# Two pairs of PSUM banks for the norm transposes, and the last image's query tiles from last to first, in a three-stage fp32 kernel

## The chip, the cores and the metric

The kernel runs on one core of one Trainium2 chip. The time is the device time of one execution in microseconds. Five engines work from queues of their own: TensorE (PE; PEld is its weight load), VectorE (DVE), ScalarE (ACT), GpSimd (POOL) and SyncE (SP), which here only issues DMA transfers. Each engine takes its instructions in the order of the program and waits at an instruction until the semaphores that it names have their value.

## The reference, cut to what matters

The input has 8 images of 256 channels and 32 x 32 pixels, all in fp32. A first layer (convolution, attention and a Fourier feed-forward part) is not touched by the change. Its result, as 1024 tokens per image, goes through a causal attention and a mixture of 8 experts:

```python
t = _to_tokens(x)                       # 8 x 1024 x 256
t = t + attention(_ln_t(t), WQ, WK, WV) # causal softmax over 1024 keys; scores equal to 0 are left out
u = _ln_t(t)                            # layer norm over the 256 channels
feat = mean(u, axis=0)                  # over the 8 images
w = softmax(feat @ Wr + br)             # a weight per token and expert
h = relu(bn(u @ W1[e])); h = relu(bn(h @ W2[e]))
y = sum_e w[e] * (h @ Wo[e] + bo[e])
x = _from_tokens(t + y)
```

The gate w needs the mean over all images, so no expert's result can be weighted before the last image's layer norm is done for those tokens.

## The kernel before, in words

Images lie channel-first: a tile t holds 2 x 128 channels (KC = 2) by 1024 tokens. The tokens are cut into two halves of 512 (HALF), eight query tiles of 128 (P) and four pairs of query tiles of 256 columns (QC).

**Layer 1's attention** (1428 to 2051 us of the span). For image b the main strand `causal` takes the query tiles 0 to 7. `scores` does eight matmul records' worth of 128x512 fp32 products into a tile s, VectorE takes the maximum (nm), and ScalarE the exponential (pr) over the causal width, 128 columns for tile 0 and 1024 for tile 7. `follow` then moves older tiles along: `norm` masks and sums on VectorE and scales on GpSimd; `turn` transposes pr on TensorE into banks "tp" and ScalarE copies them to pT; `product`, once per pair of query tiles, multiplies with the values (po), and VectorE adds po to t. The side strand `beside` runs, meanwhile, the first layer norm of image b+1, some splitting of expert weights ("chores"), the second layer norm of image b-1, and keys and values of image b+1 (pk, pv). `together` weaves the two strands by the costs that each `yield` names; this fixes the order of the program, and each engine follows it.

A layer norm (`layer_norm`, L1287) transposes pairs of token tiles on TensorE (tpt), copies them on ScalarE (zt), takes mean and variance on VectorE, the inverse root in six small steps on GpSimd, scales zt on VectorE two tiles at a time, transposes back in groups of four (tpz), and copies to z on ScalarE. For the second norm GpSimd adds the result to feats (two halves), and the result is split in parts and stored in z_d for layer 2.

PSUM in this stage: ps_s holds two score tiles (two banks each), ps_t two banks with the tag "tp", ps_m two banks with the tag "mm". pk, pv and po use "mm"; the transposes of pr use "tp". The norms and the gate take theirs from `bank`, which gives "tp" only:

```python
        def bank(shape, name):
            return ps_t.tile(shape, F32, tag="tp", name=name)
```

For the last image (b = 7) the side strand has no next image: it does the second norm of image 6, then `last_norm`, which waits until the pairs 0 and 1 are done, normalises the first half of image 7 (z2_last), adds it to feats[0], and runs `gate(0)`: logits (lg), softmax (ge) and a transpose (pwT) to wT. The second half of image 7 is normalised and gated later, inside layer 2 (`last_half`, L1822).

**Layer 2, the experts** (2051 to 3187 us). A visit is (group of four experts G, half h, image b). Each visit has four pieces, one per expert slot; a piece runs layer1 (pa, then h), two pieces later layer2 (pm), and four pieces after its start layer3 (q), so three layers run side by side. Each fp32 product is done in parts, with weights split before in wd. In the first visits of a half the gate's rows (pw) and the weighted bias (pg, `gated_bias`) are made as well. The pool `hp` and three PSUM pools open when the attention's pools close; a tile there lies over memory that the attention used. Weights are loaded by `load_expert`, tokens' parts by `fetch_z`, t by `fetch_t` (L1686), all through SP's queue in the order of the program.

Nearly all instructions of these layers carry the line of one recording helper (L72), so the profile is read by tile names.

Of the kernel before, what the change touches and what calls it, by code (L numbers as in the profile page):

```python
# [104 lines left out]
def conv_attn_hybrid_kernel(  # L105
# [1128 lines left out]
    brs = wm.tile([1, NE], F32, name="brs")  # L1234
    nc.sync.dma_start(brs, br)
    wT = wm.tile([4 * NE, N], F32R, name="wT")
    feats = [None, wm.tile([P, KC, HALF], F32, name="feat1")]
    z2_last = wm.tile([P, KC, HALF], F32, name="z2_last")
    mhalf1 = wm.tile([P, NT], F32, name="mhalf1")
    nc.gpsimd.memset(mhalf1, -0.5)  # L1240
# [124 lines left out]
    with ExitStack() as l1:  # L1365
# [19 lines left out]
            return w_  # L1385

        wv_s = load_w("wv", wvT)
        feats[0] = wpool.tile([P, KC, HALF], F32, name="feat0")
        load_t(1)


# [19 lines left out]
        def expert_parts():  # L1411

            for e in range(NE):
                for l, src in enumerate((w1, w2, wo)):
                    if not in_parts(e, l):
                        continue
                    w_ = two.tile([P, KC, C], F32, tag="we", name="we", bufs=1)
                    nc.sync.dma_start(w_, src[e].rearrange("(k p) o -> p k o", p=P))
                    yield
                    upper(parts_w, w_, dve)  # L1420
                    lower_part(parts_w, w_)
                    difference(parts_w)
                    dve.tensor_scalar_mul(parts_w[:, 1], parts_w[:, 1].bitcast(F32), STEP)
                    yield
                    nc.sync.dma_start(w_d[e][l], parts_w.bitcast(F32))
                if e == 0:
                    for k in range(3):
                        load_expert(wm, 0, k)

            consts["bn1"] = bn_fold("g1", "be1", "m1", "v1", eps_moe, "bn1", extra="b1")  # L1430
            consts["bn2"] = bn_fold("g2", "be2", "m2", "v2", eps_moe, "bn2", extra="b2")
            for i in "12":
                for x, f in (("a", 1.0 + 1.0 / STEP), ("b", -1.0 / STEP)):
                    consts[i + x] = const.tile([P, KC * NE], F32, name=f"s{i}{x}")
                    dve.tensor_scalar_mul(consts[i + x], consts["bn" + i][0], f)
            yield
            bo4 = tiny.tile([P, KC, 4, NE], F32, name="bo4", bufs=1)
            stacked(bo4, cols("bo").rearrange("p (e g) -> p g e", g=KC), (0, 0, 1, 1))
            pb = bank([4 * NE, KC, P], "pbo")
            for g in range(KC):  # L1440
                pe.transpose(pb[:, g, :], bo4[:, g].rearrange("p a e -> p (a e)"), ident)
            dve.tensor_copy(boT, pb)
            yield
            zs[0] = wm.tile([P, 3, KC, HALF], F32R, name="z_first")
            nc.sync.dma_start(zs[0].bitcast(F32), z_d[0][:, 0])
            load_expert(wm, 1, 0)
            yield

# [5 lines left out]
        def room(shape, tag, bufs):  # L1454
            return tiny.tile(shape, F32, tag=tag, name=tag, bufs=bufs)

        def bank(shape, name):
            return ps_t.tile(shape, F32, tag="tp", name=name)

        def rows_of_zt():  # L1460
# [56 lines left out]

        def last_norm():

            yield from until((B - 1, HALF // QC - 1))  # L1520
            yield from layer_norm(t[B - 1][:, :, :HALF], z2_last, rows_of_zt(), room, bank)
            dve.tensor_add(feats[0], feats[0], z2_last)
            nc.sync.dma_start(u_d[B - 1][:, :, :HALF], t[B - 1][:, :, :HALF])
            yield 0.5

        done, late, ready, turns, pr_of, pT = set(), [], [], [], {}, {}
        nq = QC // P

        def causal(b):
            for i in range(NT):  # L1530
                yield from scores(b, i)
                yield from follow()

        def follow():
            if ready:
                yield from product(*ready.pop(0))
            if late:
                norm(*late.pop(0))
            if len(turns) > 2 or (turns and not late and turns[0][0] == B - 1 and ended):
                b, i = turns.pop(0)  # L1540
                yield from turn(b, i)
                if i % nq == nq - 1:
                    ready.append((b, i // nq))

        def scores(b, i):
# [26 lines left out]
        def turn(b, i):  # L1572

            qc, qt = divmod(i, nq)
            if qt == 0:
                pT[b, qc] = two.tile([P, NT, QC], F32, tag="pT", name="pT1")
            pr = pr_of.pop((b, i))
            for j0 in range(0, i + 1, 4):
                jn = min(4, i + 1 - j0)
                tp = ps_t.tile([P, 4, P], F32, tag="tp", name="tp")  # L1580
                for j in range(jn):
                    pe.transpose(tp[:, j, :], pr[:, (j0 + j) * P : (j0 + j + 1) * P], ident)
                act.copy(pT[b, qc][:, j0 : j0 + jn, qt * P : (qt + 1) * P], tp[:, :jn, :])
                yield 0.12 * jn
# [18 lines left out]
        def beside(b):  # L1603

            def chore(n):
                for _ in range(n):
                    next(chores, None)
                    yield 1.0

            if b + 1 < B:  # L1610
                yield from first_norm(b + 1)
            yield from chore(3)
            if b >= 1:
                yield from second_norm(b - 1)
            yield from chore(2)
            if b + 1 < B:
                yield from keys_values(b + 1)
            else:
                yield from last_norm()
                yield from gate(0, room, bank)  # L1620
            yield from chore(2)

        def last():
# [12 lines left out]
            together(last() if b == B - 1 else causal(b), beside(b), 0.85)  # L1636
        for _ in chores:
            pass
        nc.sync.dma_start(u_d[B - 1][:, :, HALF:], t[B - 1][:, :, HALF:])

# [9 lines left out]


    with ExitStack() as l2:
        hp = l2.enter_context(tc.tile_pool(name="hp", bufs=2))
        ps_a = l2.enter_context(tc.tile_pool(name="ps_a2", bufs=2, space=PSUM))
        ps_b = l2.enter_context(tc.tile_pool(name="ps_b2", bufs=2, space=PSUM))
        ps_q = l2.enter_context(tc.tile_pool(name="ps_q2", bufs=1, space=PSUM))
        (s1, o1), (s2, o2) = consts["bn1"], consts["bn2"]
        s1a, s1b, s2a, s2b = (consts[x] for x in ("1a", "1b", "2a", "2b"))  # L1660

        visits = [(G, h, b) for G in range(NG) for h in range(2) for b in range(B)]
        pieces = [(v, s) for v in range(len(visits)) for s in range(SLOTS)]
        ts, gate_of, bias_of, h1_of, h2_of, acc_of = {}, {}, {}, {}, {}, {}

# [3 lines left out]
        def fetch_z(v):  # L1669
            if v < len(visits):  # L1670
                G, h, b = visits[v]
                zs[v] = hp.tile([P, 3, KC, HALF], F32R, tag="z", name="ze")
                if (G, b) == (0, B - 1):
                    parts, src = zs[v], z2_last if h == 0 else scratch[:, 2]
                    soon[0].append(lambda: upper(parts, src))
                    soon[1].append(lambda: lower_part(parts, src))
                    soon[2].append(lambda: difference(parts))
                    soon[3].append(lambda: later.append(lambda: nc.sync.dma_start(z_d[b][:, h], parts.bitcast(F32))))
                else:
                    nc.sync.dma_start(zs[v].bitcast(F32), z_d[b][:, h])  # L1680
# [120 lines left out]
                            nc.sync.dma_start(to, t)  # L1801
                    yield

        load_expert(hp, 1, 1)
        fetch_t(0)
        for s in range(1, SLOTS):
            for l in range(3):
                if (s, l) not in w_in:
                    load_expert(hp, s, l)
        fetch_z(1)  # L1810
        LAG2, LAG3 = 2, 4
        later = []
        scratch = hp.tile([P, 3, KC, HALF], F32, name="scratch", bufs=1)
# [7 lines left out]

        def last_half():  # L1822

            nc.sync.dma_start(scratch[:, 0], u_d[B - 1][:, :, HALF:])
            yield
            zt = scratch[:, 1].rearrange("p k (i c) -> p (k i) c", c=C)
            yield from layer_norm(scratch[:, 0], scratch[:, 2], zt, room2, bank2)
            dve.tensor_add(feats[1], feats[1], scratch[:, 2])
            yield
            yield from gate(1, room2, bank2)  # L1830

        extra = last_half()
        for n in range(len(pieces) + LAG3):
            one_ = two_ = three = iter(())
            if n < len(pieces):
                v, s = pieces[n]
                G, h, b = visits[v]
                if s == 1:
                    fetch_t(v + 1)
                    if v >= 1:  # L1840
                        fetch_z(v + 1)
                if s == 2 and G == 0:
                    dve.tensor_add(ts[v], ts[v], bias_of[h])
                one_ = layer1(v, s)
            if 0 <= n - LAG2 < len(pieces):
                two_ = layer2(*pieces[n - LAG2])
            if n >= LAG3:
                three = layer3(*pieces[n - LAG3])

            now, soon = soon, [[] for _ in range(4)]  # L1850
            for i in range(4):
# [8 lines left out]
            later.clear()  # L1860
            if n < len(pieces) and b == 0:
                gate_rows(G, h, s)
                if G == 0 and s < KC:
                    gated_bias(h, s)
            for l, lag in enumerate((0, LAG2, LAG3)):
                if 0 <= n - lag < len(pieces):
                    v, s = pieces[n - lag]
                    if visits[v] == (0, 1, B - 1):
                        load_expert(wm if s == 0 or (s, l) == (1, 0) else hp, SLOTS + s, l)


# [112 lines left out]
```

## Time and profile before

| | us |
|---|---|
| median of 3 runs | 3188.72 (3186.95 to 3191.35) |
| the profiled execution | 3188.79 |
| its span | 3186.8 |
| mean granted clock of TensorE | 0.966 |
| TensorE busy, 1500 to 1900 us | 379.9 of 400 |
| TensorE busy, 1963 to 2051 us (image 7 and gate) | 74.81 of 88 |
| TensorE busy, 2051 to 2100 us | 45.75 of 49 |
| TensorE busy, 2100 to 3100 us | 999.64 of 1000 |
| first scores of images 0 to 7 | 1463.76, 1517.44, 1590.68, 1665.03, 1739.31, 1813.63, 1889.42, 1963.73 |
| first matmul of layer 2 | 2050.89 |

In the lists of waits a line reads: engine and tile that waited, the engine and tile waited for, the sum in us, how often, and the longest. In the order of time a line gives start, duration, engine, line, operation, the tiles out and in, sizes, the number of instructions, and in brackets the idle time before them with what ended it. In tables by stretch each engine has its busy time and, in brackets, the count of its instructions.

### The profile page before, as it was taken

The page shows a single profiled execution, that of the slowest core. Times are in us where ns is not written, and L with a number is a line of the kernel's source. Part 1 is how long each engine was busy: PE and PEld are TensorE (multiplying, and loading weights), DVE is VectorE, ACT ScalarE, POOL GpSimd, SP SyncE. Part 2 cuts the span into 40 slices and gives each one's busy share as a digit, 9 for nine tenths or more (in the row PEclk, how much of TensorE's full clock was granted, in tenths as well). Part 3 has the DMA queues.
Part 4 walks back from the last instruction along what each step waited for, and adds up shares of the span by engine and source line. Part 5 has one row for each costly group of instructions (what it writes and reads, how often), then busy time and mean ns, then how long its engine had stood idle before and what let it go on. Part 6 is the DMA issues. An engine that isn't in the chain of part 4 may idle for free.

```text
span 3186.8 us, 41632 instructions
## 1 busy us (share of the span) xinstructions
PE 2936.5 (92%) x16802; PEld 1934.3 (61%) x16802; DVE 2390.5 (75%) x3014; ACT 1567.0 (49%) x2312; POOL 340.3 (11%) x419
## 2 busy tenths in 40 slices
PE   5998898998998989858999999799999999999998
PEld 3654555554555555435666666577777777777776
DVE  1378778878787879664677765588988888888887
ACT  1554445555554536323333332365666666666665
POOL 1121212111111110001222221100000000000000
PEclk9998999999999999979999999899999999999999
DMA  5213030302121120002433221322212242221220
GB/s 152 60 22 80 27 80 27 80 28 73 35 58 50 40 54 8 17 22 93 149 119 119 106 103 67 145 85 81 73 67 71 75 172 86 95 70 66 92 75 27
DMA packets 63854, 234.85 MB, mean 74 GB/s; under 512 B 5590, under 2 KB 13862, under 8 KB 54822
## 3 DMA queue, kind: packets, MB, share of 16 engines
q1 hardware_dynamic: 63654, 232.12, 21.9%
q8 instruction: 134, 2.20, 0.3%
q14 instruction: 66, 0.54, 0.1%
HBM read 140.61 MB, written 91.49 MB: 73 GB/s over the span
## 4 chain that ended last, share of the span: by engine, by line
PE 46%; DVE 6%; ACT 2%; issue 1%; DMA 0%; POOL 0%; SPq 0%; ACTq 0%; DVEq 0%; POOLq 0%
PE pm L72 12%; PE pa L72 11%; PE q L72 11%; PE s L72 4%; PE po L72 3%; PE pv L72 2%; PE pk L72 1%; DVE nm L72 1%; DVE zt L72 1%; DVE pr L72 1%; ACT pr L72 1%; PE tpz L72 1%; PE tpt L72 1%; DVE st L72 1%; PE tp L72 1%
## 5 line engine op out<-in xcount | busy, mean ns | idle before, releaser
L72 PE MATMUL pa<-ze,w 128*128 128x512 f32 x1488 | 423.1, 393 | 0.0
L72 DVE SCALAR_TENSOR_TENSOR x<-hpad,vec,x 128x1024 f32<-128x1024 f32 x248 | 317.0, 1282 | 40.7 <-ACT x L72 33.7
L72 DVE SCALAR_TENSOR_TENSOR conv<-hpad,vec,conv 128x1024 f32<-128x1024 f32 x256 | 329.2, 1293 | 13.8 <-ACT conv L72 7.3
L72 PEld LDWEIGHTS pa<-ze,w 128*128 128x128 f32 x1488 | 278.2, 188 | 63.3 <-issue 3.3
L72 ACT ACTIVATE h<-pa,bn_o,s1a 128x512 f32<-128x512 f32 x256 | 198.8, 777 | 204.5 <-PE pa L72 204.5
L72 ACT ACTIVATE pT<-s 128x1024 f32<-128x1024 f32 x256 | 247.5, 1025 | 71.6 <-PE s L72 71.6
L72 PE MATMUL po<-pT,vT 128*32 128x256 f32 x4096 | 272.6, 384 | 0.0
L72 PE MATMUL q<-h2p,w 128*128 128x512 f32 x768 | 269.8, 460 | 0.1
L72 DVE SCALAR_TENSOR_TENSOR h<-pa,s1b,h 128x512 f32<-128x512 f32 x256 | 191.2, 747 | 97.1 <-PE pa L72 86.6
L72 PE MATMUL ph<-xn,piw 128*128 128x512 f32 x512 | 245.2, 616 | 3.1 <-DVE xn L72 1.6
L72 PE MATMUL pm<-h,w 128*128 128x512 f32 x512 | 243.6, 598 | 0.0
L72 PE MATMUL s<-kk,z 128*128 128x512 f32 x512 | 241.3, 603 | 1.0 <-DVE pr L72 0.6
L72 PE MATMUL q<-z_first,w 128*128 128x512 f32 x768 | 216.1, 390 | 2.7 <-DVE z_first L72 1.7
L72 PE MATMUL pm<-h1p,w 128*128 128x512 f32 x768 | 216.1, 389 | 0.5 <-DVE h1p L72 0.5
L72 DVE SCALAR_TENSOR_TENSOR o<-vpad,pe_w,o 128x1024 f32<-128x1024 f32 x128 | 163.5, 1282 | 45.8 <-ACT o L72 42.7
L72 PEld LDWEIGHTS q<-h2p,w 128*128 128x128 f32 x768 | 144.7, 189 | 84.3 <-issue 60.1
L72 PE MATMUL s<-qst,kst 128*128 128x256 f32 x1024 | 176.3, 314 | 14.9 <-DMA kst<-part 13.5
L72 ACT ACTIVATE hpad<-ph,pi_o 128x512 f32<-128x512 f32 x126 | 86.9, 690 | 183.0 <-PE ph L72 182.9
L72 PEld LDWEIGHTS po<-pT,vT 128*32 128x32 f32 x4096 | 120.4, 110 | 85.0 <-issue 2.8
L72 PEld LDWEIGHTS s<-qst,kst 128*128 128x128 f32 x1024 | 137.6, 193 | 48.4 <-issue 42.7
L72 PEld LDWEIGHTS q<-z_first,w 128*128 128x128 f32 x768 | 143.8, 188 | 34.2 <-DVE z_first L72 2.9
L72 PEld LDWEIGHTS pm<-h1p,w 128*128 128x128 f32 x768 | 144.1, 188 | 31.5 <-DVE h1p L72 0.9
(268 smaller groups left out, 5063.4 us busy)
## 6 DMA issues: line engine op xcount, KB each, us to landing
ze<-zd SPq DMA_DIRECT2D x29, 1536.0 KB, 6.4
qst<-part SPq DMA_DIRECT2D x32, 512.0 KB, 8.3
kst<-part SPq DMA_DIRECT2D x32, 512.0 KB, 15.1
te<-ud SPq DMA_DIRECT2D x32, 512.0 KB, 4.1
wd<-parts_w SPq DMA_DIRECT2D x20, 768.0 KB, 3.7
w<-wd SPq DMA_DIRECT2D x20, 768.0 KB, 4.4
zd<-parts SPq DMA_DIRECT2D x14, 1024.0 KB, 4.5
t<-in_x_dram SPq DMA_DIRECT2D x8, 1024.0 KB, 5.2
```

Of the source, the lines that this page charges most:

```text
L72: return self._tc.keep_in_program_order(method(*args, **kwargs))
```

## The change

Five things change together.

1. `bank` gives "mm" and "tp" in turn, for all norms and the gate in layer 1.
2. The last image's query tiles run from 7 down to 0; `turned` counts a pair's turned tiles, since the higher tile of a pair now comes first. `last_norm` waits for the pairs 2 and 3 and normalises the second half, `gate(1)` follows it; the first half is left to `last_half` in layer 2, which so runs `gate(0)`. feats[0] goes into the long-lived pool, feats[1] into the attention's.
3. Visits run half 1 before half 0, and the first visit's parts (z_first) are those of half 1.
4. The pools of layer 2 wait for reuse by tile rather than as a whole pool, and the first loads of weights come in another order.
5. t is fetched in its own visit at slot 2 (before: one visit ahead, at slot 1), the bias is added to t at the start of layer3 of slot 2, and the weighted bias is made in the slots 2 and 3.

```diff
-    feats = [None, wm.tile([P, KC, HALF], F32, name="feat1")]
+    feats = [wm.tile([P, KC, HALF], F32, name="feat0"), None]
...
-        feats[0] = wpool.tile([P, KC, HALF], F32, name="feat0")
+        feats[1] = wpool.tile([P, KC, HALF], F32, name="feat1")
...
-            nc.sync.dma_start(zs[0].bitcast(F32), z_d[0][:, 0])
+            nc.sync.dma_start(zs[0].bitcast(F32), z_d[0][:, 1])
...
+        turns_of = [0]
+
         def bank(shape, name):
+            turns_of[0] += 1
+            if turns_of[0] % 2:
+                return ps_m.tile(shape, F32, tag="mm", name=name)
             return ps_t.tile(shape, F32, tag="tp", name=name)
...
-            yield from until((B - 1, HALF // QC - 1))
-            yield from layer_norm(t[B - 1][:, :, :HALF], z2_last, rows_of_zt(), room, bank)
-            dve.tensor_add(feats[0], feats[0], z2_last)
-            nc.sync.dma_start(u_d[B - 1][:, :, :HALF], t[B - 1][:, :, :HALF])
+            for qc in range(HALF // QC, N // QC):
+                yield from until((B - 1, qc))
+            yield from layer_norm(t[B - 1][:, :, HALF:], z2_last, rows_of_zt(), room, bank)
+            dve.tensor_add(feats[1], feats[1], z2_last)
+            nc.sync.dma_start(u_d[B - 1][:, :, HALF:], t[B - 1][:, :, HALF:])
...
-            for i in range(NT):
+            for i in range(NT) if b < B - 1 else reversed(range(NT)):
...
-                if i % nq == nq - 1:
+                turned[b, i // nq] = turned.get((b, i // nq), 0) + 1
+                if turned[b, i // nq] == nq:
...
-                yield from gate(0, room, bank)
+                yield from gate(1, room, bank)
...
-        hp = l2.enter_context(tc.tile_pool(name="hp", bufs=2))
+        hp = l2.enter_context(tc.tile_pool(name="hp", bufs=2, reuse_waits="tile"))
...
-        visits = [(G, h, b) for G in range(NG) for h in range(2) for b in range(B)]
+        visits = [(G, h, b) for G in range(NG) for h in (1, 0) for b in range(B)]
...
-        load_expert(hp, 1, 1)
-        fetch_t(0)
-        for s in range(1, SLOTS):
-            for l in range(3):
-                if (s, l) not in w_in:
-                    load_expert(hp, s, l)
+        for s, l in ((2, 0), (3, 0), (1, 1), (2, 1)):
+            load_expert(hp, s, l)
         fetch_z(1)
+        for s, l in ((1, 2), (3, 1), (2, 2), (3, 2)):
+            load_expert(hp, s, l)
...
-                if s == 1:
-                    fetch_t(v + 1)
-                    if v >= 1:
-                        fetch_z(v + 1)
-                if s == 2 and G == 0:
-                    dve.tensor_add(ts[v], ts[v], bias_of[h])
+                if s == 1 and v >= 1:
+                    fetch_z(v + 1)
+                if s == 2:
+                    fetch_t(v)
...
-                three = layer3(*pieces[n - LAG3])
+                v3, s3 = pieces[n - LAG3]
+                if s3 == 2 and visits[v3][0] == 0:
+                    dve.tensor_add(ts[v3], ts[v3], bias_of[visits[v3][1]])
+                three = layer3(v3, s3)
...
-                if G == 0 and s < KC:
-                    gated_bias(h, s)
+                if G == 0 and s >= SLOTS - KC:
+                    gated_bias(h, s - SLOTS + KC)
```

The three PSUM pools of layer 2 change as hp does; `last_half` and the last visit of a group exchange the halves 0 and 1 in the same way.

## The prediction

> **What bounds the kernel now.** I read the page's totals first, then busy time by stretch, then TensorE's waits, then the order of time around the waits that the change touches.
>
> ```profile
> PE 2936.5 (92%) x16802; PEld 1934.3 (61%) x16802; DVE 2390.5 (75%) x3014; ACT 1567.0 (49%) x2312; POOL 340.3 (11%) x419
> ```
>
> TensorE is the bound, so the change can win only where TensorE stands idle or slow, in the stretches that it touches: the attention of layer 1 (from 1428 us) and the seam into layer 2. Between 2100 and 3100 us it is busy for 999.64 of 1000 us: nothing moved there can win, and it loses only if something becomes late. The waits of TensorE, first for images 0 to 6 of layer 1 (1430 to 1964 us), then for image 7 and the seam (1963 to 2067 us):
>
> ```profile
> PE tpz L72 <- ACT pT L72: 13.6, 6, 2.3
> PE tpz L72 <- DVE zt L72: 11.4, 5, 6.2
> PE tp L72 <- ACT zt L72: 2.0, 6, 0.3
> PE tp L72 <- ACT z L72: 1.4, 6, 0.2
> ```
>
> ```profile
> PE tpz L72 <- DVE zt L72: 4.3, 3, 2.0
> PE po L72 <- ACT pT L72: 3.0, 1, 3.0
> PE pa L72 <- DMA w<-wd: 2.7, 1, 2.7
> PE pwT L72 <- DVE ge L72: 2.2, 1, 2.2
> PE lg L72 <- DVE feat L72: 1.9, 1, 1.9
> PE tpz L72 <- ACT pT L72: 1.1, 1, 1.1
> ```
>
> The 13.6 us is the wait for a bank: the norm's second transpose group (tpz) needs a "tp" bank, and the copy that frees it (pT) stands behind a 0.90 us Exp on ScalarE. One second norm in order of time:
>
> ```profile
> 1712.05 0.67 PE L72 MATMUL tpz<-ident,zt 128*128 128x128 f32 x4 [2.27 <-ACT pT L72]
> 1712.54 3.58 PE L72 MATMUL s<-kk,z 128*128 128x512 f32 x4
> 1713.15 3.98 DVE L72 TENSOR_SCALAR zt<-zt,mv,r 128x256 f32<-128x256 f32 x4
> 1714.28 2.38 POOL L72 TENSOR_TENSOR feat<-feat,z 128x1024 f32<-128x1024 f32 x1
> 1715.93 0.63 PE L72 MATMUL tpz<-ident,zt 128*128 128x128 f32 x4
> 1716.95 0.67 PE L72 MATMUL tpz<-ident,zt 128*128 128x128 f32 x4 [0.40 <-DVE zt L72]
> ```
>
> The reader sees that the fourth group (1716.95) does not hang on the bank at all. It comes 3.80 us after VectorE starts the last four scalings, and those start behind the softmax chain of a query tile (maximum, Exp, mask, sum, reciprocal; 1713.07), whatever TensorE did before. In the five second norms from 1637 us on (those of images 1 to 5) that distance is 3.80 to 3.81 us each time.
>
> Last, the granted clock (columns: stretch, its length, busy us of PE, PEld, DVE, ACT, POOL, then PEclk, DMA share, GB/s), and the product behind the fourth group, in the second norms of images 1 and 4:
>
> ```profile
> 1862.75:1866.16 3.41, 1.41 (x10) 0.91 (x9) 3.41 (x4) 0.59 (x1) 2.51 (x2) 1.00 0.00 0
> 1866.16:1869.57 3.41, 3.41 (x11) 2.79 (x10) 1.33 (x2) 2.54 (x3) 2.36 (x1) 0.50 0.02 5
> ```
>
> ```profile
> 1643.15 3.20 PE L72 MATMUL po<-pT,v 128*128 128x256 f32 x16
> 1866.07 4.88 PE L72 MATMUL po<-pT,v 128*128 128x256 f32 x16
> ```
>
> TensorE was busy for 1.41 us of one 3.41 us stretch, and got half the clock for the next: the product took 1.68 us more. The clock changes only on this grid. From 1300 us to the end, the full-clock stretches followed by half clock have busy shares of 0.41 or less, thirteen of them, with one exception (busy throughout, near 2204 us); none with 0.42 or more is otherwise followed by it.
>
> **The change, part by part.** The profiled execution took 3188.79 us (span 3186.8), the median of the runs shown is 3188.72, so the sum starts from 3188.8. Counts per engine stay as they are (layers 1 and 2: 5718 on PE, 1898 DVE, 187 POOL, 211 SP).
>
> *Banks, images 0 to 6.* The bank wait goes (6 x 2.27 = 13.6), but the next thing late is the scaling zt: TensorE runs on to the third and fourth groups and waits there until the same moment, 3.80 us after the scalings start. I take 0 for it; the ends are 0 and -13.6. The 0.33 us waits (tp <- ACT zt, 2.0 in all) lie ahead of the same moment: 0, with -2.0 as the other end. The 0.24 us waits (tp <- ACT z) come in the next image's first norm, where work and not a chain follows: -1.4. Image 0's norm, alone on TensorE, waits 0.8 and 0.46 us for z copies: about -0.5 of these. New waits: a transpose in an "mm" bank queues behind the reader of pk, pv or po. These readers (a ScalarE copy of 0.59, VectorE's add of 0.68) are short, and two uses of the ring lie between; I take 0, with 0.68 per norm and 14 norms, +9.5, as the far end.
>
> *The clock.* Before, the 4.3 us idle of a second norm lies in two pieces with 1.7 us of scores between. After, the scores have run early, and about 4.4 us idle is one stretch before the fourth group, with one group (0.6) inside. Wherever the grid falls, one window is then below 0.41, and the half-clock window reaches over the product. A half window costs up to 1.7 us; as only the part after the fourth group costs, I take 1.0 for each of 6 images, 6.0. Before paid 1.68 (norm of image 4) and about 0.5 (norm of image 0, by a score tile of 2.80 against 1.88 us that is in part taken up by the wait behind it): net +3.8, from 0 to +8.
>
> The Trainium skill ("TensorE: Matmul & The Clock Gate", HAM oscillation) says that idle gaps above about 3.4 us are what throttles. By that rule, gaps of 2.3 and 2.0 us would not throttle before, yet the rows show half clock after 1.41 us busy in 3.41; the measurement decides. By the rule the sum would end 3.8 lower, at 3179.
>
> *Image 7, tiles 7 to 0.* It runs from 1963.73 to layer 2's first matmul at 2050.89, 87.2 us, with 13.1 idle. PE order after: the last tpz groups of image 6's norm stand behind 16 po matmuls (16 x 0.4 = 6.4 us) and scores, longer than the 3.98 of zt: 1.08 and 2.00 go. The 2.96 before po of the widest pair goes, as tile 7 now comes first and its chain (maximum 1.2, Exp 1.1, mask 0.29, sum 1.2, scale 1.14, transposes 0.9, copies 0.9) lies beside other tiles. What is late next is the narrow tiles' chain at the end: for tiles 1 and 0 maximum 1.2, Exp 0.4, mask 0.3, sum 0.4, reciprocal 0.3, scale 0.3, copy 0.3, about 3.2, against 1.7 (tpt, tp, score remnants) on TensorE: 1.5 for the pair 3-2, and 0.7 for the pair 1-0. The last norm's own chain (zt copy 0.59, statistics 2 x 0.6, POOL 2.5, zt 0.73) waited 1.76 and 0.57; after it, the last product (8 matmuls, 1.3) lies partly beside it, as 32 did before: 1.0 and 0.7. Two tp waits (0.4, 0.6) replace 0.35 and 0.23. Before: 1.08 + 2.00 + 2.96 + 1.76 + 0.57 + 0.35 + 0.23 = 8.95. After: 1.5 + 0.7 + 1.0 + 0.7 + 0.4 + 0.6 = 4.9. That is -4.0. The waits for feat (1.94) and ge (2.18) stay, and the logits stay at half clock. The ends: -9 if no narrow tile is waited for, 0 if each costs what the widest did. On SP the half's store (512 KB) now stands ahead of the loads, as the other half's did; VectorE's two half adds swap places.
>
> *Seam.* Before, every load of layer 2 waits for the whole attention pool: the first goes out at 2051.38, and expert 2's first weights, fourth in the queue, are waited for 2.66 us; the window at 2064.13 is then at half clock (3.41 / 2 = 1.7). After, the loads wait for single tiles, and that weight is first. It overlays feats[1], so it waits for the end of the logits, about 3 us ahead of the first matmul; 768 KB takes 4.4 us (the page's median), and it is needed 8 to 10 us after. So 2.66 + 1.7 go. What hid ScalarE's h copies in pieces 0 and 1 (pg, 2 x 0.33) moves to pieces 2 and 3: back +1.0 (three waits like the 0.40 seen). Net -3.3; the ends are 0 and -4.4. The moved t loads (512 KB, 4.1 us) and bias adds lie beside TensorE's full stretch: a visit's t is used at its third layer, some 4 pieces later. Cost 0; if that cover fails, 4.1 us once per late load.
>
> Sum: 3188.8 - 1.4 - 0.5 + 3.8 - 4.0 - 3.3 = 3183.4.
>
> **The rivals.** *The bank wait was the limit.* For it: the profile names it, 13.6 us, with a separate wait for zt. Then 15.6 us go (with the 2.0), the idle gathers nowhere, and 3188.8 - 15.6 - 1.4 - 0.5 - 4.0 - 3.3 = 3164. Against: the fixed 3.80 us. If zt itself came half as early, about 3174.
>
> *The clock is worse (slower).* If two half windows follow each gathered gap, 3.4 us x 6 = 20.4, less the 2.2 paid before: +18.2 for +3.8, 3197.8. It decides from a cost of about 3.0 us per norm. For: the gap of 4.4 is longer than a window. Against: a second window needs a share below 0.41 while the product runs in it.
>
> *Tail and seam give nothing.* The narrow tiles' chains cost all of the 4.0, and the queue still lands weights late: 3188.8 - 1.9 + 3.8 = 3190.7. For: the tail's exposed chain from last product to logits is the same length in both. Against: the 2.96 had one cause, tile width.
>
> **How the numbers follow.** About 0.2% (6.4 us) is what a measurement of this kernel can tell from no change: 3182.4 and 3195.2 are the bounds. My forecast 0.60, with its own range of 3177 to 3190; 0.27 of it falls below 3182.4 and 0.33 within. Bank limit 0.15, faster. Tail and seam nothing 0.12, same. Clock 0.13, of which 0.12 slower (with an "mm" wait at its far end). Faster 0.42, same 0.46, slower 0.12. The range leaves out the first rival's full case and the upper part of the clock's: 3172 to 3195.
>
> **What would show it.** tpz <- ACT pT gone between 1430 and 1964 us, and tpz <- DVE zt grown by about as much; the fourth group still 3.8 us after the scalings; half-clock windows behind every second norm, po at 3.2 to 4.9 us; image 7 some 83 us from its first score to the first pa; no DMA wait in the first pieces. It is wrong if zt starts earlier, if tp, tpt or tpz waits for VectorE's adds, if the layer 2 stretch is no longer full, or if pa waits for a later weight.

## The result and the profile after

The changed kernel took 3183.36 us (median of 17 runs, 3178.24 to 3187.12), the kernel before, beside it, 3191.35 us (17 runs, 3182.26 to 3201.76). The ratio is 0.9978, with a 95% interval of 0.9970 to 0.9985: 5 to 10 us less. The forecast was 3183.4. The 0.2% that the prediction took for the bound of "no change" lies inside the interval, so the gain is clear of zero and not clear of that bound.

The profiled execution spans 3181.8 us. Cut at the same places as before (first scores of an image, first matmul of layer 2), in us:

| | before | after | forecast of the step |
|---|---|---|---|
| up to the first scores | 1463.8 | 1466.4 | -0.5 |
| images 0 to 6 | 500.0 | 501.4 | +2.4 |
| image 7 with the gate | 87.2 | 80.7 | -4.0 |
| layer 2 | 1135.9 | 1133.3 | -3.3 |
| span | 3186.8 | 3181.8 | -5.4 |

The first row's +2.7 lies in layer 0, which the change does not touch: its last product (votes) started at 1421.0 us before and at 1423.7 after. Image 0's norm, from its first transpose to the first scores, took 27.1 and 27.0 us; the wait for a DMA ahead of that transpose (tpt <- DMA at) took 15.4 and 15.5 us. Behind layer 0 the changed kernel is 7.7 us shorter.

TensorE's waits in the changed kernel, from 1430 us to image 7:

```profile
PE tpz L72 <- DVE zt L72: 29.9, 20, 6.7
PE tpt L72 <- DMA at<-at_d: 15.5, 1, 15.5
PE s L72 <- DVE pr L72: 4.1, 7, 0.6
PE tpz L72 <- ACT z L72: 0.7, 1, 0.7
PE tp L72 <- ACT z L72: 0.2, 1, 0.2
```

The 15.5 us are the wait ahead of image 0's norm, 15.4 before. The 13.6 us for a bank are gone, and the wait for zt has grown from 11.4 to 29.9 us. A wait that was not forecast came with it: s <- DVE pr, 0.58 us in each of six images, since TensorE now runs far enough ahead to need the next score tile early. One second norm of the changed kernel in order of time, and the clock over the same stretch (columns as before: length, busy us of PE, PEld, DVE, ACT, POOL, PEclk, DMA share, GB/s):

```profile
1714.88 3.98 DVE L72 TENSOR_SCALAR zt<-zt,mv,r 128x256 f32<-128x256 f32 x4
1715.33 0.44 PE L72 MATMUL tpz<-ident,zt 128*128 128x128 f32 x2 [1.66 <-DVE zt L72]
1716.01 2.37 POOL L72 TENSOR_TENSOR feat<-feat,z 128x1024 f32<-128x1024 f32 x1
1716.24 0.44 PE L72 MATMUL tpz<-ident,zt 128*128 128x128 f32 x2 [0.48 <-DVE zt L72]
1718.68 1.09 PE L72 MATMUL tpz<-ident,zt 128*128 128x128 f32 x4 [2.00 <-DVE zt L72]
1719.56 4.45 PE L72 MATMUL po<-pT,v 128*128 128x256 f32 x16
```

```profile
1715.26:1718.67 3.41, 0.88 (x4) 0.42 (x5) 3.41 (x4) 0.58 (x1) 3.12 (x2) 1.00 0.00 0
1718.67:1722.09 3.42, 3.41 (x10) 2.91 (x11) 1.32 (x2) 2.28 (x3) 1.62 (x1) 0.50 0.00 0
```

The fourth group still comes 3.80 us after the scalings start (1714.88 to 1718.68). The idle lies in one stretch, the next window has half clock, and the product takes 4.45 us instead of 3.20.

The waits from image 7 to the first pieces of layer 2:

```profile
PE pwT L72 <- DVE ge L72: 2.2, 1, 2.2
PE lg L72 <- DVE feat L72: 2.0, 1, 2.0
PE po L72 <- ACT pT L72: 2.0, 2, 1.4
PE pg L72 <- ACT wb L72: 0.7, 1, 0.7
PE tpz L72 <- DVE zt L72: 0.7, 1, 0.7
PE pa L72 <- ACT h L72: 0.4, 1, 0.4
PE tp L72 <- ACT pT L72: 0.3, 1, 0.3
PE tp L72 <- ACT z L72: 0.3, 1, 0.3
```

Against the list of before, 4.3 us for zt fell to 0.7, the 3.0 us for one wide pT became 2.0 for two narrow ones, and the wait for a weight is gone. What the gate needs (feat, ge) is waited for as before.

### The profile page after: what moved, and what is told of

The parts are those of the page before. It is cut to its first block, busy times and chain, and to the rows that moved or that the text cites. A ratio compares the mean times of both kernels' runs of the same rounds, so it can differ in the third digit from the quotient of the medians.

```text
span 3181.8 us, 41598 instructions
## 1 busy us (share of the span) xinstructions
PE 2935.8 (92%) x16802; PEld 1938.8 (61%) x16802; DVE 2390.2 (75%) x3014; ACT 1565.1 (49%) x2312; POOL 341.0 (11%) x419
## 4 chain that ended last, share of the span: by engine, by line
PE 49%; DVE 4%; ACT 1%; issue 0%; POOL 0%; SPq 0%; DMA 0%; ACTq 0%; DVEq 0%
PE pm L72 12%; PE pa L72 11%; PE q L72 11%; PE s L72 4%; PE po L72 4%; PE pv L72 2%; PE pk L72 2%; DVE zt L72 1%; DVE nm L72 1%; PE tp L72 1%; DVE pr L72 1%; PE tpz L72 1%; PE tpt L72 1%; DVE st L72 1%; ACT pr L72 1%
```

## The experiments

The theory: the alternation of banks moves a wait and does not remove it, because the scalings zt set the norm's end and the idle then halves the clock; the gain comes from image 7, a little from the seam. The main rival: the bank wait was the limit, and its removal is the gain. The cuts of all profiles, in us:

| | images 1 to 6 | image 7 and gate | layer 2 | span |
|---|---|---|---|---|
| before | 446.3 | 87.2 | 1135.9 | 3186.8 |
| changed | 447.8 | 80.7 | 1133.3 | 3181.8 |
| e1 banks alone | 447.8 | 88.8 | 1136.2 | 3188.3 |
| e2 reversal alone | 446.2 | 81.9 | 1134.3 | 3178.2 |
| e3 seam alone | 448.2 | 88.8 | 1134.3 | 3190.9 |
| e4 changed, no alternation | 446.9 | 81.9 | 1133.9 | 3181.1 |
| e5 changed, adds swapped | 440.6 | 79.4 | 1133.8 | 3169.5 |
| e6 before, adds swapped | 445.6 | 89.0 | 1136.1 | 3188.0 |
| e7 = e4, adds swapped | 448.3 | 80.8 | 1133.6 | 3178.1 |
| e8 changed, filled | 442.9 | 80.7 | 1133.7 | 3174.9 |
| e9 = e5, filled | 439.1 | 79.5 | 1133.7 | 3172.5 |
| e10 = e9, gate filled | 439.2 | 79.8 | 1131.7 | 3171.2 |
| e11 before, filled | 448.8 | 90.2 | 1132.7 | 3190.5 |
| e12 = e3, filled | 450.1 | 88.7 | 1131.8 | 3190.5 |

Spans also carry layer 0's own spread: the first scores came between 1461.8 and 1467.0 us in these profiles. Layer 2 has a spread too: before, e1, e6 and e11 share its instructions and took 1132.7 to 1136.2 us, so 2 or 3 us of one profile there say little about an edit. What varies is how much of the work falls into half-clock windows.

### e1: the alternation alone

```diff
         def bank(shape, name):
+            turns_of[0] += 1
+            if turns_of[0] % 2:
+                return ps_m.tile(shape, F32, tag="mm", name=name)
             return ps_t.tile(shape, F32, tag="tp", name=name)
```

> Only the alternation of banks, all else as before. Theory (the scalings zt set the fourth group, and gathered idle halves the clock): the 13.6 us of tpz <- ACT pT vanish and come back as waits for zt; images 2 to 6 take about 75.0 us each from first score to first score against 74.3 before, images 0 to 6 together 501 against 500; total unchanged or 1 to 2 us slower. Rival (the bank wait was the limit): images 1 to 6 shorter by 2.3 us each, 13 us faster in all.

Measured: ratio 1.0013 [1.0004, 1.0023]. Images 2 to 6 took 75.15, 74.92, 75.00, 75.27 and 75.16 us. The rival's 13 us are not there; alone, the alternation costs. Part of this profile's loss lies in image 7, 88.8 us: its wait before the widest po was followed by a half-clock window, which the profile of before happened not to have:

```profile
2017.89:2021.30 3.41, 0.45 (x2) 0.42 (x3) 2.13 (x4) 1.86 (x3) 1.01 (x1) 1.00 0.77 295
2021.30:2024.71 3.41, 3.41 (x10) 2.66 (x9) 3.24 (x6) 0.00 (x0) 1.91 (x1) 0.50 0.17 67
```

e3, e6, e11 and e12, all with the old order of tiles, show image 7 at 88.7 to 90.2 us as well. So 87.2 was the lucky case.

### e2: the reversal alone

The parts 2 and 3 of the change without 1, 4 and 5:

```diff
-            for i in range(NT):
+            for i in range(NT) if b < B - 1 else reversed(range(NT)):
...
-        visits = [(G, h, b) for G in range(NG) for h in range(2) for b in range(B)]
+        visits = [(G, h, b) for G in range(NG) for h in (1, 0) for b in range(B)]
```

> Only the reversed query tiles of the last image with the halves exchanged. Theory: images 0 to 6 as before (500 us), image 7 with the gate 81 to 83 us against 87.2 before and 80.7 in the changed kernel, layer 2 as before (1135.9): 4 to 6 us faster. Rival (the reversal needs the extra banks, since twelve transposes of the norm come in one block): image 7 stays above 85 us and the time within 2 us of before.

Measured: ratio 0.9980 [0.9971, 0.9990], as much as the whole change. Image 7 took 81.9 us. From image 7 to the first pieces:

```profile
PE po L72 <- ACT pT L72: 2.0, 2, 1.4
PE lg L72 <- DVE feat L72: 1.9, 1, 1.9
PE pa L72 <- DMA w<-wd: 1.9, 1, 1.9
PE tpz L72 <- DVE zt L72: 0.8, 1, 0.8
```

The reversal does not need the extra banks. Its layer 2 was also 1.6 us shorter, with the loads as before: the wait for a weight was 1.9 instead of 2.7 us, and no half-clock window followed it. The first two lines are e2, the others before:

```profile
2043.87 5.52 PE L72 MATMUL pa<-z_first,w 128*128 128x512 f32 x12
2056.24 1.17 PE L72 MATMUL pa<-z_first,w 128*128 128x512 f32 x4 [1.88 <-DMA w<-wd]
2050.89 4.71 PE L72 MATMUL pa<-z_first,w 128*128 128x512 f32 x12
2063.22 1.29 PE L72 MATMUL pa<-z_first,w 128*128 128x512 f32 x4 [2.66 <-DMA w<-wd]
2064.32 3.49 PE L72 MATMUL pm<-h,w 128*128 128x512 f32 x4
```

The weight was not earlier: the first load went out 0.49 us after the first pa in both. TensorE came later, since 0.8 us more went into the first twelve pa at half clock. The 1.6 us are the half-clock window over pm (3.49 us before, 1.88 in e2), so they depend on how the windows fall and can't be put down to the reversal.

### e3: the seam alone

The parts 4 and 5 without 1 to 3:

```diff
-        hp = l2.enter_context(tc.tile_pool(name="hp", bufs=2))
+        hp = l2.enter_context(tc.tile_pool(name="hp", bufs=2, reuse_waits="tile"))
...
+        for s, l in ((2, 0), (3, 0), (1, 1), (2, 1)):
+            load_expert(hp, s, l)
+        fetch_z(1)
```

> Only the reuse of memory by tile, the order of loads, the later fetch of t and the later bias. Theory: layer 1 as before (image 7 with the gate 87.2), no wait of pa for a weight, layer 2 at 1133 to 1134 us against 1135.9: 2 to 3 us faster. Rival (the loads still stand behind the end of layer 1): the 2.7 us DMA wait stays, and the waits of pg for ScalarE add 1.4 us, so 1 to 2 us slower.

Measured: ratio 1.0012 [1.0002, 1.0022], slower. The step itself did what was expected: the wait for the weight is gone, pg waits 1.4 us, and layer 2 took 1134.3 us, 1.6 less. Yet the time rose where the theory had it fall, and the rival's reason, a DMA wait that stays, is not there. The profile lost time in layer 1, whose instructions on TensorE, VectorE and ScalarE it shares with the kernel before: in three of its images a half-clock window fell on work (75.5 us against 74.3), and image 7 took 88.8. Whether that is the chance of one profile is taken up in e11 and e12.

### e4: the changed kernel without the alternation

```diff
         def bank(shape, name):
-            turns_of[0] += 1
-            if turns_of[0] % 2:
-                return ps_m.tile(shape, F32, tag="mm", name=name)
             return ps_t.tile(shape, F32, tag="tp", name=name)
```

> The changed kernel without the alternation of banks. Theory: images 0 to 6 at 500 us as before instead of 501.4, image 7 up to 1.5 us longer than 80.7, total within 2 us of the changed kernel's. Rival (the alternation carries the gain): 5 us or more slower than the changed kernel.

Measured: ratio 0.9980 [0.9971, 0.9990], against 0.9978 [0.9970, 0.9985] with it. Images 1 to 6 are 0.9 us shorter, image 7 is 1.2 longer. Within the intervals the alternation is worth nothing here. Two effects cancel: with it the fourth group comes 51.46 us after the image's first score instead of 51.93, and a half-clock window then costs something in each of the images 2 to 6, where without it two of them paid (75.6 and 75.7 us, the others 74.3).

### e5, e6, e7: what holds the scalings

In e5 GpSimd's two adds of the second norm go in the other order, so that none runs beside the last scalings; e6 is the same edit in the kernel before, e7 in e4:

```diff
-            for h, feat in enumerate(feats):
-                half = z2[:, :, h * HALF : (h + 1) * HALF]
+            for h in (1, 0):
+                feat, half = feats[h], z2[:, :, h * HALF : (h + 1) * HALF]
```

> The changed kernel with GpSimd's two adds of a second norm in the other order, second half first, so that no add runs beside the last four scalings zt. Theory (the scalings set the fourth group, and they take 3.98 us because the 2.4 us add runs beside them): the four scalings take about 1.5 us (twice 0.73), the fourth group comes 1.4 us after their start, images 2 to 6 take 72.5 to 73.5 us instead of 75.05, the time is 8 to 13 us below the changed kernel's. Rival (the scalings are long for a reason of their own): images as in the changed kernel, same time.

> The kernel before with the same swap of GpSimd's two adds, the norms on one pair of banks. Theory: the bank wait of 2.27 us stays, the 2.00 us wait for zt goes, images 2 to 6 take 72.0 to 72.8 us instead of 74.3, the time is 9 to 12 us below before. Rival (the two waits are one, and whichever engine is late the sum stays): images at 74.3, same time.

> The changed kernel without the alternation of banks and with the swap of the adds. With the scalings short the bank wait of 2.27 us can decide. Theory (the softmax chain sets the start of the scalings either way): images 2 to 6 within 0.5 us of those of the kernel before with the swap, 72.0 to 72.8, and the time within 3 us of the changed kernel with the swap. Rival (the alternation pays once the scalings are short): images 2 us longer than in the changed kernel with the swap, 12 us slower than it.

Measured: e5 3171.7 us, ratio 0.9951 [0.9936, 0.9966]; e6 1.0001 [0.9991, 1.0011]; e7 0.9969 [0.9958, 0.9981]. One norm of e5 in order of time:

```profile
1709.73 1.95 DVE L72 TENSOR_SCALAR zt<-zt,mv,r 128x256 f32<-128x256 f32 x4
1710.18 0.44 PE L72 MATMUL tpz<-ident,zt 128*128 128x128 f32 x2 [1.67 <-DVE zt L72]
1711.10 1.08 PE L72 MATMUL tpz<-ident,zt 128*128 128x128 f32 x6 [0.48 <-DVE zt L72]
1712.01 4.88 PE L72 MATMUL po<-pT,v 128*128 128x256 f32 x16
1712.88 5.66 POOL L72 TENSOR_TENSOR feat<-feat,z 128x1024 f32<-128x1024 f32 x2 [1.99 <-ACT z L72]
```

The same four scalings take 1.95 us instead of 3.98, so it was the add beside them that held them, and with them the norm. Instruction by instruction, one scaling took 0.40 us alone, 1.00 beside GpSimd's scaling of pr and 2.42 beside the add; the 1.95 us still hold one of 1.00, which is why they are not the 1.5 that was expected. The Trainium skill ("GPSIMD Engine Reference", Key points) says that GpSimd shares its SBUF interfaces with VectorE and contends with VectorE instructions that run in a 2-port mode or read two SBUF inputs. These rows show such a contention, with a factor of two; in which mode the scalings run they do not show.

With the scalings short the alternation pays: images 1 to 6 take 448.3 us without it (e7) and 440.6 with it (e5), and e5 took 3167.15 to 3174.69 us where e7 took 3176.47 to 3183.06. About 0.4 us an image is the bank's own (73.82 us in the one image of e7 from 2 on that met no half-clock window, 73.4 in e5); the rest is the clock, since the other four took 75.2 to 75.5 us. This refutes the forecast for e7: its rival, that the alternation then pays, came true at 7.7 us where it named 12. In the kernel before (e6) the same edit gives nothing at all. The waits of e6 say why:

```profile
PE tpz L72 <- ACT pT L72: 13.6, 6, 2.3
PE pk L72 <- ACT kk L72: 8.8, 5, 1.8
```

The 2.00 us for zt went, the bank wait stayed, and a wait of pk for ScalarE's copy kk came in its place, 1.8 us in each of five images. The two adds now run in one stretch, and VectorE's mask product beside them is stretched in its turn. In e6, first without and then with the adds beside it:

```profile
1709.77 0.29 DVE L72 TENSOR_TENSOR pr<-pr,lower 128x128 f32<-128x128 f32 x1 [1.03 <-ACT pr L72]
1715.95 5.67 POOL L72 TENSOR_TENSOR feat<-feat,z 128x1024 f32<-128x1024 f32 x2 [3.43 <-ACT z L72]
1719.93 1.85 DVE L72 TENSOR_TENSOR pr<-pr,lower 128x128 f32<-128x128 f32 x1
```

The next maximum and Exp stand behind that product, and kk stands behind the Exp. Besides, in three of the images 2 to 6 of e6 the bank wait of 2.27 us was followed by half clock: they took 75.25 to 75.36 us, the other two 73.86. The theory had 72.0 to 72.8 us an image, the rival 74.3; the rival had the time right and the images wrong. Three images of e5 have the wait of pk too, of 1.7 us; of images 2 to 6 the other two have a half-clock window in its place, and all five take 73.4 to 73.9 us.

### e8: the idle time filled

```diff
             tp = bank([P, KC, 2, P], "tpz")
+            for _ in range(fill.get(i0, 0) if n == NT else 0):
+                pe.matmul(tp.rearrange("p k i c -> p (k i c)"), ident, src[:, 0, :HALF], start=True, stop=True)
...
-            yield from layer_norm(t[b], z2, rows_of_zt(), room, bank)
+            yield from layer_norm(t[b], z2, rows_of_zt(), room, bank, {4: 1, 6: 2} if b < B - 2 else {})
```

> The changed kernel with idle TensorE time filled: ahead of the third tpz group of a second norm (images 0 to 5) one extra 128x512 fp32 product and ahead of the fourth two, 0.86 us each at full clock, written to the group's own bank and overwritten by its transposes; the result is not used. Theory (gathered idle halves the clock for the next 3.41 us): no half-clock window behind these norms, po x16 at 3.2 us, images 2 to 6 at 74.0 to 74.3 us instead of 75.05, 4 to 6 us faster than the changed kernel. Rival (the clock costs nothing, the chain does): images stay at 75.0 or grow by the extra work.

Measured: 3170.79 us, ratio 0.9952 [0.9939, 0.9965]. TensorE does more and the kernel is faster:

```profile
1710.66 1.02 PE L72 MATMUL tpz<-t,ident 128*128 128x512 f32 x2
1713.69 1.88 PE L72 MATMUL tpz<-t,ident 128*128 128x512 f32 x4
1715.77 0.76 PE L72 MATMUL tpz<-ident,zt 128*128 128x128 f32 x4 [0.20 <-DVE zt L72]
1716.37 3.20 PE L72 MATMUL po<-pT,v 128*128 128x256 f32 x16
```

No half-clock window follows any second norm, po takes 3.20 us, and images 2 to 4 take 73.87, 73.85 and 73.87 us instead of 74.99, 75.04 and 75.05. So the clock costs the changed kernel 1.2 us per norm, and 0.9 in image 6 (75.20 against 74.33). The profiles put 4.9 us of the gain into images 1 to 6.

### e9 and e10: both together, and the gate

e9 is e5 with one extra product ahead of the third group ({4: 1}); e10 also fills the gate:

```diff
+        busy(2)
         lg = bank([P, nt, NE], "lg")
...
+        busy(2)
         pwT = bank([4 * NE, HALF], "pwT")
```

> The changed kernel with the adds swapped and one extra 128x512 product (0.86 us) ahead of the third tpz group of each second norm of images 0 to 5, its result not used. Two theories on what is left: if the clock still costs after the swap (two of five images had a half-clock window behind the norm), images 2 to 6 fall from 73.4 to 72.5 to 73.1 us and the time by 2 to 5 us against the swap alone (3171.7). Rival (since the swap the images are set by the adds, 5.66 us on GpSimd with the splitting behind them, and pk waits for it): images stay at 73.4, time within 2 us.

> As e9, and in the gate of the last half two extra products ahead of the logits and two ahead of pwT, 1.7 us each, into an unused score tile. Theory (the logits run at half clock only because TensorE idles ahead of them): the logits take about 3 us instead of 5.9, the first pa x12 under 4 us instead of 5.4, 3 to 5 us less than e9. Rival (the logits' 8-column products are too little work to hold the clock): logits again near 5.9 us, time within 1 us of e9, or 1 us more where the extra work is late.

Measured: e9 ratio 0.9950 [0.9937, 0.9963], e10 0.9943 [0.9929, 0.9956]. In e9 the half-clock windows behind the norms are gone, and images 2 to 6 stay at 73.4 to 73.9 us: the wait of pk takes the place of the slow clock in all five. So the rival won. In e10 the first logits ran at full clock, yet the next window was slow:

```profile
2031.20:2034.61 3.41, 3.10 (x23) 2.88 (x22) 0.29 (x1) 0.00 (x0) 0.00 (x0) 1.00 0.00 0
2034.61:2038.02 3.41, 3.41 (x8) 1.81 (x8) 1.53 (x9) 0.23 (x1) 0.00 (x0) 0.50 0.59 202
```

That window was filled with logits, 8 columns each, at a busy share of 0.91. Layer 2 became 2 us shorter: 4.2 us of its first pa ran at half clock in e9 and 1.9 in e10, and behind the second gate's logits e9 had two half-clock windows and e10 one. The timed difference between e9 and e10 lies within the intervals. e5, e8, e9 and e10 beat both kernels; e5 does it without extra work.

### e11 and e12: the clock in the kernel before, and the seam again

e11 puts two extra products ahead of the fourth group of the kernel before, with the loop of e8; e12 does the same in e3:

```diff
-            yield from layer_norm(t[b], z2, rows_of_zt(), room, bank)
+            yield from layer_norm(t[b], z2, rows_of_zt(), room, bank, {6: 2} if b < B - 1 else {})
```

> The kernel before with two extra 128x512 products (1.7 us, result not used) ahead of the fourth tpz group of each second norm, in its 2.00 us wait for zt. Theory (kernels with one pair of banks pay the clock too, more or less as the windows fall): no half-clock window behind these norms, images 2 to 6 at 74.3 us each in every execution, image 5 without its extra 1.5, time 1 to 4 us below before. Rival (before pays nothing but the waits): same time as before, within 1 us.

> The same fill in the kernel with the seam's edits alone (reuse by tile, order of loads, late t, late bias). Theory (e3 was slower only because half-clock windows fell on its norms): 1 to 3 us below e11, layer 2 at 1134 us against 1136. Rival (the seam's edits cost time by themselves): 2 us or more above e11, with layer 2 above 1136 us.

Measured: e11 ratio 1.0004 [0.9995, 1.0013], e12 1.0011 [1.0002, 1.0020]. The fill failed its purpose: the 2.27 us bank wait alone is enough for the half clock, as in this window of e11 and the one behind it:

```profile
1860.75:1864.16 3.41, 1.14 (x9) 0.75 (x8) 2.35 (x5) 1.82 (x3) 0.00 (x0) 1.00 0.00 0
1864.16:1867.57 3.41, 3.41 (x7) 1.43 (x6) 3.34 (x7) 0.64 (x2) 2.44 (x2) 0.50 0.00 0
```

Three norms of e11 (those starting in images 1, 5 and 6) and four of e12 met it. Layer 2 is shorter with the seam's edits (1131.8 against 1132.7), and the time is not. e3 timed the seam's edits alone at 0.1% slower; e12 lies 0.07% above e11, which is within the intervals and settles nothing. The profiles put no such loss into layer 2. Where it lies stays open: images 1 to 6 took 446.3 us before and 448.2 in e3 with the same instructions, and single profiles cannot tell a shift from the fall of the windows.

## Why the prediction was right, point by point

- *Banks, 0 for the bank wait.* Right, for the reason given. The bank wait went, the wait for zt took its place, the fourth group stayed 3.80 us after the scalings, and e1 shows no gain in time. The rival "the bank wait was the limit" fell. e5 adds what the prediction did not work out: about 2.0 of the 3.98 us were the price of one GpSimd add, and the alternation had a value once that was gone.
- *The small waits (-1.4, -0.5).* The 0.24 us waits went from 1.4 to 0.2. This is the term of the sum that was too small: in images 1 to 5 the last scalings, and with them the fourth group, came 0.46 us earlier (47.66 us instead of 48.12 after the image's first score) where 0.24 was counted. That is 2.3 us instead of 1.4, about the 1.0 us by which the forecast for images 0 to 6 (+2.4) missed the measured +1.4. The new 0.58 us wait of s for the softmax stood nowhere in the sum. Image 0's norm before its first scores gained 0.1, not 0.5.
- *New waits in the "mm" banks, 0.* Right: no transpose waits for VectorE's adds.
- *The clock, +3.8.* The mechanism held, and the net was as forecast, in part by luck: five norms of six had the half-clock window, not every one, at 0.9 to 1.2 us each (5.6 in all against e8) where six at 1.0 were taken. The kernel before paid about 1.8 (image 5 took 75.79 us against 74.50 in e3, image 1 73.24 against 72.74) where 2.2 was taken. That leaves an estimate of +3.8. The rival with two half windows per gap did not occur: no norm had more than one. (The sum without the clock's 3.8, which the prediction gives as 3179, is 3179.6; here too half clock came behind gaps of 1.66, 0.48 and 2.00 us.) The step that failed is the bound of 0.41: in e5 windows with busy shares near 0.5 were followed by half clock, and in e10 one with 0.91. The exception near 2204 us was the key: it holds the logits of the second gate. In twelve of the fourteen profiles these 8-column products filled 0.69 to 0.90 of one window and half clock followed; in e11 and e12 the grid cut them in two (0.41 and 0.58, 0.51 and 0.48) and none followed, with TensorE busy throughout each time. So busy time of the records is not what the clock follows where the products are small. Low busy share was a sufficient sign in this kernel, no more: after 1300 us a full-clock window with 0.40 or less was followed by half clock every time in all profiles, and from 0.41 to 0.54 both occur.
- *Image 7, -4.0.* The mechanism held, the size was short: -6.5 in the profiles. The two narrow waits were 1.4 and 0.6 (1.5 and 0.7 taken). The last norm's first tpz group did not wait at all (1.0 taken), and the tp waits were 0.3 and 0.3 (0.4 and 0.6). That makes 3.2 us of waits instead of 4.9. Most of the rest is busy time: TensorE's same 327 records took 73.3 us instead of 74.0. Against the usual 88.7 to 90.2 us of the old order the gain is nearer 7: the half-clock window behind the 2.96 us wait, which the one profile of before lacked, was not in the sum.
- *Seam, -3.3.* -2.6 in the profiles, but most of it came from elsewhere: e2, with the old loads, has 1.6 of it, because no half-clock window fell on its pm. With the edits e4 was 0.4 us shorter than e2. The wait for the weight went in every profile with the edits, as forecast; that the time followed is not shown, since e3 was not faster. The waits of pg were 1.4 us (1.0 taken), and the half clock of the logits lasted into the first pa, 5.40 us for twelve where the profile of before had 4.71.

So the total of 3183.4 met 3183.36 by luck as well as by its terms. Image 7 gave more, the seam's own edits less. And the sum started from 3188.8 where the kernel before, beside the changed one, took 3191.35: the forecast difference was 5.4 us, the measured one 8.0 between the medians. In one respect the prediction had the weight right: nearly all of the gain belongs to the reversed tiles.

## What to carry to other kernels

When a wait is to be removed, ask first what the work behind it would then wait for: here a chain with a fixed distance (3.80 us) to another engine's start showed that the bank was not the limit, and only with that chain shortened did the banks pay. An elementwise instruction that takes twice its usual time has a neighbour: look at what GpSimd does in that moment. And the order of the last pieces is cheap to change: run the longest chain first where nothing follows to hide it.

## What the runs showed that was not expected

- Three useless products per norm (2.9 us of TensorE in the rows of e8) made the kernel 0.26% faster than the changed kernel (0.9952 against 0.9978), because they kept the clock (no half-clock window behind any norm, po 3.20 us).
- The changed kernel's images stayed in step with the clock's grid: the half-clock windows behind five norms began at 1643.58, 1718.67, 1793.77, 1868.86 and 1943.95 us, 75.09 us apart, which is 22 windows of 3.41 us, and the images took 75.0 us. These windows began 51.35, 51.45, 51.50, 51.54 and 51.36 us after the first score of their image, so each caught the same product. That the slow clock itself holds the images in step is a reading that no run tested. The Trainium skill ("TensorE: Matmul & The Clock Gate", Part 1) calls the window free-running, of 3413 ns; these rows agree with that, and show a loop that stays in step with it.
- The scalings took 3.98 us with a GpSimd add beside them and 1.95 without; later in e6 a 0.29 us mask product took 1.85 us for the same neighbour.
